# Splitting the weights of two hidden units for single-pass Hadamard products

## The chip, the core and the metric

The kernel runs on one core of a Trainium2 chip. The metric is the device time of one launch in microseconds (us): the median of three runs.

## What is computed

Eight sequences of 512 tokens with 512 features go through a layer norm, and from there along two ways whose results are multiplied.

```python
xn = _layernorm(x)
s = attention(xn)     # q, k, v; elu + 1; running sum of phi_k * v over the tokens; times phi_q; Wo
g = silu(ffn(xn))
return x + s * g

def ffn(x):                                        # HIDDEN 512, INTER 2048
    x = fwht(x * SU_ug) / SCALE
    x_up   = x @ W_up.T   * (Wscale_ug[:INTER] * SCALE)
    x_gate = x @ W_gate.T * (Wscale_ug[INTER:] * SCALE)
    x = silu(x_gate) * x_up
    x = fwht(x * SU_dp) / SCALE
    return x @ W_down.T * (Wscale_dp * SCALE)
```

`fwht` is a Walsh-Hadamard transform over the features. It is linear, so the kernel applies it to the weights once and not to the tokens. For a weight with 512 input features, held as four blocks of 128, it consists of butterflies between the blocks (additions and subtractions) and of a product with a 128 by 128 matrix `had` of +1 and -1 within each block.

## The kernel before

**Tiles and stages.** The tokens are taken in four passes `p` of two sequences each. All products are in float32. Each large product is done by a scheme of seven smaller ones (factors P1 to P7) on sums and differences of blocks. The operands of those factors are "encoded" by additions on VectorE or GpSimd, both for tokens and for weights. Pass 0 loads the raw weights, folds the transform into them, encodes them, uses them, and stores them to DRAM; passes 1 to 3 load the ready factors.

**Units.** The 2048 hidden features are cut into `NU` = 4 units `u`. Each unit needs the gate weights `f = u` and `u + 4` and the up weights `u` and `u + 4`. In pass 0 the units 0, 1 and 2 run through `gate` and `up` (lines 775 to 810), with weights made just ahead. Unit 3 uses `hidden_unit` (line 812) with a further level of the scheme, and its weights are made during the first `down` by `weights_ahead` (line 1061). `down` (line 858) runs after units 1 and 3.

**Making one folded weight** is `folded_w` (line 929). `raw_w` issues four loads on SP's queue. Then three steps are placed in time: `butterflies` (four VectorE operations of 128x512, lines 940 to 944), `fold` (two TensorE products of 128x512 with `had`, line 950, each result brought back from PSUM to the weight's tile by two ScalarE operations, line 955) and `encode` (four VectorE operations of 128x256, lines 312 to 315). The list at line 965 holds a place for each step: 5, 7 and 9.

**What sets the order.** The program is recorded in an order that `at` (line 429) and `advance` (line 434) make: a place is counted in TensorE products, and every step is recorded when its place has come. `get_w` (line 1112) places the steps of the next two weights: for the very next weight all of them, for the one behind it the first half. `later` and `pace` (lines 75 to 83) put side work behind groups of VectorE operations. Then a scheduler orders the instructions of each engine by priorities; on each engine they run strictly in that order. Products marked `keep_in_program_order` keep their place. SP issues the DMAs, one queue, in order too.

**Buffers.** `t8` is a pool of six tiles of 8 KB a partition, which gates, ups, attention operands, block outputs (`dn`, whose two tiles are stored to DRAM as `d_d` at the end of the first `down`) and the tiles of `weights_ahead` share. A new tile takes a slot that is free in the scheduler's view and waits for what last used it. `wpool` holds four weights. `xin` has one slot, in which the additional factors of the stored weights (`s_gate`, `s_up`, line 412) and the tokens of later sequences (`x`) follow each other. PSUM tag `t` has two banks, for the products with `had`; the folding of the down weights (`pwd`, line 1001) uses them too.

**Places that the prediction speaks of.** Line 460: the products of `gate` and `up` (`px_gate`, `pz_up` and so on; `px`, `py` and `pz` are PSUM banks). Line 476: VectorE's sums that read a `py` or `pz` bank (`g`, `u`). Line 470: ScalarE's copies of a `px` bank. Line 536: the products of `down`. Line 638: those of `hidden_unit`; line 648 the sums behind them. Line 93: the operations that `later` put off, here sums for the down weights (`rd`, `wd`). Line 140: the layer norm of the fourth sequence's tokens. Lines 710 and 711: ScalarE's elu of `q` (`neg_q`). Line 752: the store of `dn`.

Of the kernel before, what the change touches and what calls it, by code (L numbers as in the profile page):

```python
# [7 lines left out]

F32 = mybir.dt.float32
AF = mybir.ActivationFunctionType  # L10
ALU = mybir.AluOpType
PSUM = bass.MemoryType.PSUM
# [9 lines left out]
def kernel(  # L22
# [27 lines left out]
    nc = tc.nc  # L50
    P = 128
# [6 lines left out]
    NU = NG // 2  # L58
# [4 lines left out]
    const = ctx.enter_context(tc.tile_pool(name="const", bufs=1))  # L63
# [4 lines left out]
    t8 = ctx.enter_context(tc.tile_pool(name="t8", bufs=6))  # L68
# [5 lines left out]
    @contextmanager  # L74
    def background(behind=150):

        at = tc.cur_priority
        tc.cur_priority = at + behind
        yield
        tc.cur_priority = at  # L80
# [20 lines left out]

    cols_sb = const.tile([P, cols.shape[1]], F32, tag="cols", name="cols_sb")
    offs = {}
# [10 lines left out]

    bo_r = const.tile([P, D], F32, tag="bo_r", name="bo_r")
    ident = const.tile([P, P], F32, tag="ident", name="ident")
    had = const.tile([P, P], F32, tag="had", name="had")
    ones = const.tile([P, 1], F32, tag="ones", name="ones")
    su_ug = const.tile([P, KD], F32, tag="su_ug", name="su_ug")
    su_dp = const.tile([P, NF], F32, tag="su_dp", name="su_dp")  # L120
# [13 lines left out]
    def layernorm(b, xt, parts=1):  # L134
        n = NT // parts
        for i in range(0, NT, n):
# [6 lines left out]
            nc.vector.tensor_scalar(rstd, mv[:, :, 1], EPS, None, ALU.add)  # L143
            nc.scalar.activation(rstd, rstd, AF.Sqrt)
            nc.vector.reciprocal(rstd, rstd)
# [6 lines left out]
    def first_layernorms(xs):  # L152
# [8 lines left out]
        def pinned(ins):  # L161
            tc.keep_in_program_order(ins)

        for i in range(2 * NT + 1):
            if i < 2 * NT:
# [4 lines left out]
                pinned(nc.vector.tensor_scalar(r, mv[:, i, 1:2], EPS, None, ALU.add))  # L170
                nc.scalar.activation(r, r, AF.Sqrt)
            if i:
# [3 lines left out]
                if i <= NT:  # L176
                    pinned(nc.vector.scalar_tensor_tensor(n, m, -1.0, r, ALU.mult, ALU.mult))
                    nc.scalar.activation(x, x, AF.Identity, bias=n, scale=r)
                else:
# [3 lines left out]
    def normalized(b):  # L183
# [20 lines left out]
        def root():  # L204
            nc.vector.tensor_scalar(rstd, mv[:, :, 1], EPS, None, ALU.add)
            nc.scalar.activation(rstd, rstd, AF.Sqrt)

# [102 lines left out]
    def encode_weights(eng, w):  # L310
        w = w.rearrange("p j s e -> p s j e") if len(w.shape) == 4 else w
        eng.tensor_tensor(w[:, P5], w[:, P7], w[:, P4], ALU.add)
        eng.tensor_tensor(w[:, P6], w[:, P5], w[:, P1], ALU.subtract)
        eng.tensor_tensor(w[:, P3], w[:, P2], w[:, P6], ALU.subtract)
        eng.tensor_tensor(w[:, P7], w[:, P1], w[:, P7], ALU.subtract)
# [30 lines left out]
    def raw_w(name, src, n0, dn, step, c0, dc, w=None):  # L346

        w = new_w(name) if w is None else w
        for a in range(2):
            tiles = src[:, c0 + a * dc : c0 + a * dc + P].rearrange("(n p) e -> p n e", p=P)  # L350
            for b in range(2):
                n = n0 + b * dn
                place = (P1, P2, P7, P4)[2 * a + b]
                nc.sync.dma_start(w[:, :, place, :], tiles[:, n : n + step + 1 : step])
        return w
# [94 lines left out]
    def group(name, ws, rhs, dst, then, bias=(None, None), time=1.7):  # L450
# [14 lines left out]
        def snapshot(what, i):  # L465
# [5 lines left out]
            else:  # L471
                nc.scalar.activation(s, p, AF.Identity, bias=b)
            return s
# [218 lines left out]
    def attention(p, xo, co, get_w):  # L692
        def project(m, g, then):
# [4 lines left out]
            def whole(px):  # L698
                nc.scalar.activation(r[:, 0, 1], px, AF.Identity, bias=b[0])
                then(r)  # L700
# [225 lines left out]
    def folded_w(name, src, f, room=None):  # L926

        w = raw_w(f"{name}_{f}", src, 0, 2, 1, f * P, NG * P, room)
        places = (slice(P1, P7 + 1, 2), slice(P2, P4 + 1, 3))
        flat_w = w.rearrange("p j s e -> p (j s) e")  # L930

        def spots(at, *dims):
            o = flat_w[:, at : at + 1, :]
            return bass.AP(o.tensor, o.offset, [o.ap[0]] + [[step * P, 2] for step in dims] + [[1, P]])

        rs = [spots(0, 4, 2), spots(3, 8, 2)]

        def butterflies():
            a, b = (w[:, :, place, :] for place in places)
            nc.vector.tensor_tensor(spots(3, 7, 2), a, b, ALU.subtract)  # L940
            nc.vector.tensor_tensor(a, a, b, ALU.add)
            a, b = spots(0, 3, 2), spots(7, 3, 2)
            nc.vector.tensor_tensor(spots(4, 7, 2), a, b, ALU.subtract)
            nc.vector.tensor_tensor(a, a, b, ALU.add)

        def fold():
            for b in range(2):
                p = ps.tile([P, 2, 2, P], F32, tag="t", name=f"pw_{name}_{f}_{b}")
                tc.keep_in_program_order(
                    nc.tensor.matmul(  # L950
                        p, had, rs[b], start=True, stop=True,
                    )
                )
                for j in range(2):
                    nc.scalar.activation(
                        w[:, j, places[b], :], p[:, j], AF.Copy, scale=su_ug[:, 2 * b + j : 2 * b + j + 1]
                    )
        def encode():
            encode_weights(nc.vector, w)
            folded[name, f] = w  # L960
            if f >= NU:
                with background():
                    inner_w(name, f - NU, folded[name, f - NU], w)

        return w, [(5, butterflies), (7, fold), (9, encode)]

    folded = {}
    wd_f = dram.tile([FF, D], F32, tag="wd_f", name="wd_f")
# [74 lines left out]
    def first_w(m, g):  # L1043


        if m == "gate":
            return folded_w(m, wgate_t, g)
        if m == "up":
            return folded_w(m, wup_t, g)
        name, eng = f"{m}_{g}", nc.gpsimd if m == "o" else nc.vector  # L1050
        if m == "o":
            t = new_w(name)
            w = by_factor(t)
            rows_w(w, wo_t, g, 2)
        else:
            t = w = raw_w(name, sources[m], 0, 2, 1, g * P, 2 * P)

        def encode():
            encode_weights(eng, w)
            keep_w(name, t)  # L1060

        return w, [(5, encode)]
# [79 lines left out]
    had2 = t8.tile([P, P], F32, tag="t", name="had2")  # L1142
    src = ident
    for i in range(7):
        dst = had if i % 2 == 0 else had2
        s = src.rearrange("p (a t h) -> p a t h", t=2, h=1 << i)
        d = dst.rearrange("p (a t h) -> p a t h", t=2, h=1 << i)
        nc.gpsimd.tensor_tensor(d[:, :, 0, :], s[:, :, 0, :], s[:, :, 1, :], ALU.add)
        nc.gpsimd.tensor_tensor(d[:, :, 1, :], s[:, :, 0, :], s[:, :, 1, :], ALU.subtract)
        src = dst  # L1150
    xo = xop.tile([P, 7, 7, H], F32, tag="xo", name="xo_0")
    first_layernorms(xs)
    for b in range(2):
# [11 lines left out]
    rs = rd[:, : 3 * NF * P].rearrange("p (i c e) -> p i c e", i=3, e=P)  # L1165
# [141 lines left out]
```

## Time and profile before

| | |
|---|---|
| median of three runs | 1553.38 us (1552.45 to 1556.04) |
| the profiled execution | 1554.91 us |
| its span, first to last instruction | 1553.1 us |
| granted TensorE clock, mean | 0.999 |
| ScalarE busy (ACT) | 419.8 us (27%) |
| GpSimd busy (POOL) | 432.6 us (28%) |
| DMA | 273.31 MB, mean 176 GB/s |

The profile gives for each engine the time in which an instruction ran. Matmuls are pipelined, so the length printed for one is longer than the distance to the next; the distance between starts tells what a product costs. "PEld" are the weight loads of TensorE, which run beside its products. A row of a timeline has the start in us from the span's beginning, the length of the merged group, the engine, the line, the operation, the tiles, the shape and the count; in brackets, how long the engine was idle just before and what ended that. One float32 product of the program appears as two MATMUL records in the trace.

In pass 0, units 0 to 2 run from about 85 to 365 us. The products with `had` of the second unit (u = 1) lie between 181 and 225 us, those of `weights_ahead` between 263 and 286 us, and those of the third unit (u = 2) between 306 and 341 us.

### The profile page before, as it was taken

What the parts mean: (1) busy time and instruction counts of PE and PEld (TensorE: products, weight loads), DVE (VectorE), ACT (ScalarE), POOL (GpSimd) and SP (SyncE); (2) the same over time, 40 slices, a digit from 0 to 9 for tenths busy, and PEclk for the clock granted to TensorE, in tenths of its full rate; (3) what the DMA queues carried; (4) which work ended last, traced back from release to release, by engine and by line L of the source; (5) the groups of instructions that cost most, each with busy time, mean ns of one, the idle gap of its engine ahead of it and who ended that gap; (6) DMA issues with size and microseconds to landing.
All of it is one profiled execution on the core that took longest, in us unless ns stands there. A gap on an engine that the chain in (4) does not pass through costs nothing.

```text
span 1553.1 us, 15703 instructions
## 1 busy us (share of the span) xinstructions
PE 1524.6 (98%) x5924; PEld 1121.6 (72%) x5924; DVE 1006.7 (65%) x1423; ACT 419.8 (27%) x664; POOL 432.6 (28%) x236
## 2 busy tenths in 40 slices
PE   7989999999999999999999999999999999999998
PEld 3436446746874588888884488888886478888887
DVE  7989787467877665616767674715675575533673
ACT  4453341232125411112114431111213431111211
POOL 1231233004320161305511144302621126210731
PEclk9999999999999999999999999999999999999999
DMA  8345867797975244354576344335574233535462
GB/s 276 97 155 162 268 231 227 224 307 241 270 277 164 86 158 156 99 164 164 166 265 228 100 143 149 114 118 184 178 244 154 91 109 105 189 102 173 162 256 84
DMA packets 197692, 273.31 MB, mean 176 GB/s; under 512 B 56816, under 2 KB 155120, under 8 KB 193392
## 3 DMA queue, kind: packets, MB, share of 16 engines
q1 hardware_dynamic: 197472, 272.27, 53.3%
q8 instruction: 47, 0.77, 0.2%
q14 instruction: 29, 0.24, 0.1%
q10 hardware_dynamic: 144, 0.03, 0.0%
HBM read 196.25 MB, written 76.02 MB: 175 GB/s over the span
## 4 chain that ended last, share of the span: by engine, by line
PE 88%; DVE 7%; DMA 3%; ACT 1%; issue 1%; SPq 0%; POOL 0%; POOLq 0%; DVEq 0%; ACTq 0%
PE px_gu L638 19%; PE px_dn L536 13%; PE pz_gu L638 10%; PE pz_dn L536 7%; PE py_gu L638 5%; PE px_k L460 4%; PE py_dn L536 4%; PE px_o L536 4%; PE px_v L460 3%; PE px_q L460 3%; PE pz_o L536 2%; PE px_up L460 2%; PE pz_k L460 2%; PE pz_v L460 2%; PE pz_q L460 2%; PE px_gate L460 1%
## 5 line engine op out<-in xcount | busy, mean ns | idle before, releaser
L638 PE MATMUL px_gu<-xo,w_gu 128*128 128x256 f32 x1456 | 347.8, 380 | 2.4 <-DVE sb_gu L648 2.2
L638 PEld LDWEIGHTS px_gu<-xo,w_gu 128*128 128x128 f32 x1456 | 275.7, 190 | 47.3 <-issue 5.0
L536 PE MATMUL px_dn<-w_down,ho 128*128 128x256 f32 x1024 | 228.5, 379 | 0.0
L536 PEld LDWEIGHTS px_dn<-w_down,ho 128*128 128x128 f32 x1024 | 194.6, 190 | 28.2 <-issue 1.9
L638 PE MATMUL pz_gu<-xo,w_gu 128*128 128x256 f32 x728 | 187.7, 380 | 2.1 <-DVE u L476 1.6
L838 POOL TENSOR_TENSOR u<-u,v 128x1024 f32<-128x1024 f32 x26 | 61.0, 2369 | 366.3 <-DVE u L676 347.4
L638 PEld LDWEIGHTS pz_gu<-xo,w_gu 128*128 128x128 f32 x728 | 137.5, 190 | 23.3 <-DVE u L476 2.0
L536 PE MATMUL pz_dn<-w_down,ho 128*128 128x256 f32 x496 | 114.2, 383 | 3.4 <-DVE u L476 3.4
L536 PEld LDWEIGHTS pz_dn<-w_down,ho 128*128 128x128 f32 x496 | 95.0, 193 | 18.7 <-DVE u L476 3.8
L638 PE MATMUL py_gu<-xo,w_gu 128*128 128x256 f32 x364 | 93.4, 379 | 0.0
L304 POOL TENSOR_TENSOR co<-co 128x512 f32<-128x512 f32 x8 | 14.8, 1848 | 266.2 <-DVE co L737 266.2
L883 POOL TENSOR_TENSOR s<-s,d 128x512 f32<-128x512 f32 x30 | 40.0, 1335 | 165.5 <-ACT d L882 165.5
L638 PEld LDWEIGHTS py_gu<-xo,w_gu 128*128 128x128 f32 x364 | 69.2, 190 | 9.4
L842 POOL TENSOR_TENSOR v<-v,r 128x1024 f32<-128x1024 f32 x26 | 60.9, 2366 | 26.3 <-DVE r L676 25.5
L460 PE MATMUL px_k<-xo,w_k 128*128 128x512 f32 x128 | 62.2, 609 | 0.0
L460 PE MATMUL px_v<-xo,w_v 128*128 128x512 f32 x128 | 60.6, 594 | 0.0
L460 PE MATMUL px_q<-xo,w_q 128*128 128x512 f32 x128 | 60.3, 592 | 0.0
L828 ACT ACTIVATE a<-a,cols_sb 128x512 f32<-128x512 f32 x26 | 18.8, 724 | 152.2 <-DVE a L676 150.3
L882 ACT ACTIVATE d<-d 128x512 f32<-128x512 f32 x31 | 19.6, 632 | 144.4 <-DVE d L551 114.2
L536 PE MATMUL px_o<-w_o,co 128*128 128x256 f32 x256 | 58.4, 379 | 0.0
L828 ACT ACTIVATE u<-u,cols_sb 128x512 f32<-128x512 f32 x52 | 37.0, 722 | 78.1 <-DVE u L676 68.1
L536 PE MATMUL py_dn<-w_down,ho 128*128 128x256 f32 x256 | 57.9, 379 | 0.0
(269 smaller groups left out, 2416.2 us busy)
## 6 DMA issues: line engine op xcount, KB each, us to landing
w_gu<-d_gu SPq DMA_DIRECT2D x91, 896.0 KB, 4.4
w_down<-d_down SPq DMA_DIRECT2D x56, 512.0 KB, 4.1
d_s<-o SPq DMA_DIRECT2D x8, 1024.0 KB, 5.7
d_d<-dn SPq DMA_DIRECT2D x8, 1024.0 KB, 7.6
d<-d_d SPq DMA_DIRECT2D x8, 1024.0 KB, 5.6
s<-d_s SPq DMA_DIRECT2D x8, 1024.0 KB, 7.5
y<-in_x_dram SPq DMA_DIRECT2D x8, 1024.0 KB, 6.9
out_dram<-y SPq DMA_DIRECT2D x15, 512.0 KB, 3.3
```

The source lines that it names most:

```text
L304: eng.tensor_tensor(o[..., P5, :], o[..., P7, :], o[..., P1, :], ALU.subtract)
L460: nc.tensor.matmul(p.rearrange("p a t -> p (a t)") if len(r.shape) == 2 else p, ws[k][:, i, :], r, start=(first and k == 0), stop=(k == n ...
L536: nc.tensor.matmul(p[:, c], t[:, (2 * g + c) * P : (2 * g + c + 1) * P], ws[i](k), start=(first and k == 0 and c == cs[0]), stop=(k == n - ...
L638: nc.tensor.matmul(p[:, lane], w[:, lane, i, :], x[:, i, :], start=(first and lane == 0), stop=True, skip_group_check=True,)
L828: nc.scalar.activation(g[:, m], g[:, m], AF.Silu, scale=col("w_gate", u + m * NU + a * NG))
L838: nc.gpsimd.tensor_tensor(r[:, m], ru1[:, m], rv[:, m], ALU.add)
L842: nc.gpsimd.tensor_tensor(rv[:, m], rv[:, m], rr[:, m], ALU.add)
L882: nc.scalar.activation(d, d, AF.Silu)
L883: (nc.vector if final and (a, s) == (1, 0) else nc.gpsimd).tensor_tensor(r, r, d, ALU.mult)
```

## The change

For the weights with `f % 4` equal to 1 or 2 (gate and up weights 1, 2, 5 and 6, eight in all), the step `butterflies` also splits the result into two parts. ScalarE copies it into a tile of type float32r, which rounds it; VectorE subtracts the rounded part from the full one and writes the rest as float32r. Each half of the weight becomes two products with `had` in float32r, summed in PSUM. `had` holds +1 and -1, which are exact in that type, so its tile is declared float32r and read as float32 elsewhere. The two parts lie in a tile from the pool `t8`. For all folded weights, the second place of the list goes from 7 to 8.

```diff
-    had = const.tile([P, P], F32, tag="had", name="had")
+    had_r = const.tile([P, P], F32R, tag="had", name="had")
+    had = had_r.bitcast(F32)
...
+        parts = []
 
         def butterflies():
             a, b = (w[:, :, place, :] for place in places)
...
             nc.vector.tensor_tensor(a, a, b, ALU.add)
+            if f % NU in (1, 2):
+                t = t8.tile([P, 2, 2, 4 * P], F32R, tag="t", name=f"r_{name}_{f}")
+                for b in range(2):
+                    high, low = (
+                        t[:, b, i].rearrange("p (j a e) -> p j a e", j=2, a=2) for i in range(2)
+                    )
+                    nc.scalar.copy(high, rs[b])
+                    nc.vector.tensor_tensor(low, rs[b], high.bitcast(F32), ALU.subtract)
+                    parts.append(t[:, b])
+
+        def by_had(p, b):
+            if not parts:
+                tc.keep_in_program_order(nc.tensor.matmul(p, had, rs[b], start=True, stop=True))
+                return
+            for i in range(2):
+                tc.keep_in_program_order(
+                    nc.tensor.matmul(
+                        p.rearrange("p j a e -> p (j a e)"), had_r, parts[b][:, i], start=(i == 0), stop=(i == 1)
+                    )
+                )
 
         def fold():
             for b in range(2):
                 p = ps.tile([P, 2, 2, P], F32, tag="t", name=f"pw_{name}_{f}_{b}")
-                tc.keep_in_program_order(
-                    nc.tensor.matmul(
-                        p, had, rs[b], start=True, stop=True,
-                    )
-                )
+                by_had(p, b)
...
-        return w, [(5, butterflies), (7, fold), (9, encode)]
+        return w, [(5, butterflies), (8, fold), (9, encode)]
```

## The prediction, made before the changed kernel ran

> **What bounds the kernel now.** I read the shares of busy time first, then the chain of work that ended last, then what TensorE (PE) waited for in the window 60 to 400 us, in which the edit lies, and last the timelines of the engines at those waits. From the page:
>
> ```profile
> PE 1524.6 (98%) x5924; PEld 1121.6 (72%) x5924; DVE 1006.7 (65%) x1423; ACT 419.8 (27%) x664; POOL 432.6 (28%) x236
> ...
> PE 88%; DVE 7%; DMA 3%; ACT 1%; issue 1%; SPq 0%; POOL 0%; POOLq 0%; DVEq 0%; ACTq 0%
> ```
>
> TensorE is the bound, and the chain lies on it for 88%. So a product that is shortened is a gain, unless TensorE then waits. VectorE (DVE) is at 65% on average and ScalarE (ACT) at 27%; but the edit gives VectorE work in pass 0, and there it is the releaser of TensorE's waits. These, with the total, the times and the longest in us:
>
> ```profile
> PE pz_dn L536 <- DVE u L476: 3.4, 1, 3.4
> PE px_gate L460 <- DVE w_gate L313: 2.5, 2, 2.0
> PE px_gu L638 <- DVE sb_gu L648: 2.2, 1, 2.2
> ...
> PE pwd L1001 <- ACT w_gate L955: 1.7, 1, 1.7
> ```
>
> They sit at 258.71, 99.74, 381.88 and 106.83 us; a fifth, of 0.51, at 207.29. Each ends what an edit ahead of it gains or loses: where VectorE sets the end, TensorE coming earlier only waits longer.
>
> **The products.** TensorE's timeline:
>
> ```profile
> 194.60 1.88 PE L950 MATMUL pw_gate<-w_gate,had 128*128 128x512 f32 x4
> 196.32 1.88 PE L460 MATMUL pz_up<-xo,w_up 128*128 128x512 f32 x4
> ...
> 207.29 1.95 PE L460 MATMUL px_gate<-xo,w_gate 128*128 128x512 f32 x4 [0.51 <-DVE w_gate L313]
> ...
> 249.10 2.75 PE L536 MATMUL pz_dn<-w_down,ho 128*128 128x256 f32 x12
> ...
> 258.71 4.54 PE L536 MATMUL pz_dn<-w_down,ho 128*128 128x256 f32 x12 [3.41 <-DVE u L476]
> ...
> 381.88 1.13 PE L638 MATMUL px_gu<-xo,w_gu 128*128 128x256 f32 x4 [2.17 <-DVE sb_gu L648]
> ```
>
> The two products of one weight with `had` take 196.32 - 194.60 = 1.72 us, in four records of 0.43. No row shows a single-pass product of 128x512. Its price c is above that of a record with a quarter of the columns (the transposes of line 271: 128x128, four in 0.44, so 0.11) and not above one record of the same columns, 0.43. I take the middle, 0.27. A weight then costs 4 x 0.27 = 1.08 in place of 1.72: 0.64 less; eight weights 5.1 us less. With 0.11 it would be 10.2 less, with 0.43 nothing.
>
> The Trainium skill, page "FP8 and Floating Point Precision", section TensorE Precision Notes, says that true FP32 is done in four passes over high and low parts, and that reduced FP32 is read and truncated to FP22; from 0.86 us for a product, c would be about 0.215 (an estimate), the saving 6.9 and the sum below 0.7 lower.
>
> **The added work.** For a weight, two ScalarE copies of 128x512: the like copies of line 470 take 0.59 each, so 1.2 together. Two VectorE subtractions of 128x512: line 944 has 0.69 long and 0.60 from start to start, so 1.2. That is 9.6 us on each engine, in the units 1 and 2. What they cost is where they stand in the queues; I laid the changed program's instruction order against the times of before.
>
> *Unit 0, up to 110 us (no weight is split, but place 7 becomes 8): +0.9.* TensorE gets one more product of unit 0 ahead of `pw_gate_0`, so the wait at 99.74 (2.04) shortens to about 1.4. Then `pw_gate_4`'s second half needs the PSUM bank that ScalarE clears of `pwd_0`, and this eviction now stands behind the four `neg_q` operations: free at about 112.3, where TensorE comes at 107.8. So a wait of about 4.5 takes the place of the 1.70 at 106.83 and of two others (2.04 and 0.70, less the 1.4 left). 4.5 + 1.4 - 4.44 = 1.5, of which reordered products give back some; `py_gate_4` starts at 117.5 by my walk, 116.66 before: +0.9.
>
> *Unit 1, 110 to 260 us: +2.3 at its end.* VectorE and SP's queue (line 354 loads the raw weight, line 404 stores factors):
>
> ```profile
> 201.23 4.51 DVE L93 TENSOR_TENSOR rd<-rd 128x1024 f32<-128x1024 f32 x2
> 205.66 1.48 DVE L313 TENSOR_TENSOR w_gate<-w_gate 128x256 f32<-128x256 f32 x1
> ...
> 239.89 1.09 DVE L412 TENSOR_TENSOR s_up<-w_up 128x896 f32<-128x896 f32 x1 [3.67 <-DMA d_gu<-s_gate]
> ```
>
> ```profile
> 190.89 0.93 SPq L404 DMA_DIRECT2D d_gu<-s_up  x1
> 191.91 2.77 SPq L354 DMA_DIRECT2D w_up<-in_wup_t_dram  x4
> ```
>
> The 0.9 of unit 0 and the four subtractions of `r_gate_1` and `r_gate_5` (2.4), less about 1.0 of idle time that takes them up, put VectorE's `s_up` and so SP's store at 190.89 later by 2.3; the four loads of `w_up_1` stand behind it in the queue, so they land at 200.0 for 197.7. In the changed order the encoding of `w_gate_5` (205.66) stands behind two `rd` sums, the four butterflies of `w_up_1`, and the subtractions of `r_up_1`, which wait for ScalarE's copies: done at 211.9 for 207.1. TensorE needs it at 205.9, so the wait of 0.51 becomes about 6.0. The same delay runs on through x's layer norm, whose store on SP is at 224.7 (227.6 after, +2.9), to the chain of `xin`'s one slot: `s_gate`, its store, `s_up` (the 3.67 at 239.89), the loads behind it on SP, VectorE's butterflies of `w_gate_3`, and `u` (line 476), which releases `pz_dn` at 258.71. There `u` stands one operation (0.6) further ahead in the queue: 258.71 + 2.9 - 0.6 = 261.0, +2.3. TensorE comes at 257.7 (255.3 before), so what its cheaper products in unit 1 saved only lengthens or shortens a wait. If idle time takes up all additions, the end is -0.6; if it takes up none of the unit's eight subtractions (4.8), 0.9 + 4.8 - 0.6 = +5.1.
>
> The clock: after the wait of 3.41 the twelve `pz_dn` records take 4.54 where they take 2.75 at 249.10; the granted clock (PEclk, ninth column group) goes to 0.97 and 0.95:
>
> ```profile
> 160.00:180.00 20.00, 20.00 (x50) 9.33 (x50) 12.93 (x20) 9.41 (x28) 1.82 (x2) 1.00 0.90 298
> 240.00:260.00 20.00, 16.59 (x61) 11.76 (x60) 16.72 (x19) 1.76 (x3) 9.18 (x5) 0.97 0.94 284
> 260.00:280.00 20.00, 20.00 (x77) 15.10 (x77) 13.49 (x24) 5.57 (x13) 1.46 (x1) 0.95 0.57 164
> ```
>
> That is a loss of about 1.7. After the 2.04 at 99.74 there is none. The new waits of 4.5 and 6.0 may each cost 1.7 too, but both lie ahead of places where VectorE sets the end and TensorE has idle time to lose it in; and the wait at 258 stays near 3.3. So I add nothing, and keep +1.7 for the range.
>
> The skill's page "TensorE: Matmul & The Clock Gate", section Part 1: The HAM clock gate, speaks against the change here: by it an idle window of about 3.4 us halves the clock until a busy one has passed. The row of 4.54 for 2.75 agrees with a dip after 3.41; by the rule both new waits would bring one, by the rows only those beyond 2.04 might.
>
> *Unit 2, 300 to 345 us: -1.4.* `r_gate_2` takes the slot of a block output whose store is issued on SP at 300.49 and lands in 4.7 to 5.1 us (median 4.9), so at 305.4. Two copies and the last subtraction end at 307.4 to 308.1; TensorE comes at 306.21. Its waits, and the copies for `r_gate_6` that stand between the evictions of `pw_gate_2`'s two halves, make the factors behind come at 310.2 for 309.65: +0.55. The other three weights find their parts ready: 3 x 0.64 = -1.92. With c = 0.11 the sum is -3.3, with 0.43 it is +0.65.
>
> *Unit 3: -2.0.* At 381.88 TensorE waited 2.17 for `sb_gu`, which stood in VectorE's queue behind a layer norm that waited for its tokens:
>
> ```profile
> 379.95 1.29 DVE L140 BATCH_NORM_STATS2 st<-x 128x6 f32<-128x512 f32 x2 [3.48 <-DMA x<-in_x_dram]
> ```
>
> In the changed order those statistics come behind `sb_gu`, so that the wait goes. What is late next there is VectorE's own sums: about 0.2. If the wait stays, nothing is gained.
>
> *Behind 400 us* the order hardly changes, and TensorE waits little. **Sum**: +2.3 - 1.4 - 2.0 = -1.1 against the profiled execution (1554.91, span 1553.1 and 1.8 around it): 1553.8. The median of the runs, 1553.38, is 1.5 below that execution; the same -1.1 gives **1552.3**.
>
> **The rivals.** What a measurement can tell from no change is about 0.2%, 3.1 us.
>
> A, the forecast: the second unit swallows its gain, the third and fourth keep theirs. 1552.3, within 0.2%. Chance 0.36.
>
> B, faster: VectorE's idle time (35% on average) takes up all the additions in unit 1, so that the chain to `pz_dn` is not longer: -0.6 - 1.4 - 2.0 = -4.0, 1549.4. With c at 0.11, 1.9 less: 1547.5. For it: before its `s_up` VectorE waits 3.67 for a store. Against: that store is itself behind VectorE's earlier work. Chance 0.32.
>
> C, slower: VectorE's queue in unit 1 has no room where the chain needs it, so that all eight subtractions delay `u` and with it `pz_dn`, +5.1; and in unit 3 VectorE's own sums are late in place of the statistics, so that the 2.0 don't come: +5.1 - 1.4 = +3.7, 1557.1. It decides once the chain is later by more than 4.5 with nothing gained in unit 3 (4.5 - 1.4 = 3.1). For it: four of the five waits named end on VectorE, and its operations get longer beside others (line 313 took 1.48 at 205.66). Against: VectorE's idle time before `s_up`. Chance 0.26.
>
> D, the change doesn't do what it says: a product of the short type takes one record's 0.43, so that two cost as much as the float32 one: +2.3 + 0.65 - 2.0 = +0.95, 1554.3, within 0.2%. Chance 0.06.
>
> **The numbers.** Faster is B, 0.32; within 0.2% is A and D, 0.42; slower is C, 0.26. The range goes from B with the cheapest product, 1547.5, to just beyond C, 1558.0 (half of a clock dip of 1.7). A's own range is 1550.4 (c = 0.11) to 1556.1 (c = 0.43 and a dip: 2.05 + 1.7).
>
> **What would show it.** c is the distance of starts of the `had` products, against 0.43 a record. The walk is right if TensorE waits some 4.5 us for the bank at `pw_gate_4` near 108, some 6 for line 313's `w_gate` near 206, and still 3 to 4 at `pz_dn` near 258, resumed about 261; if `pw_gate_2` waits 1 to 2 us for VectorE's subtraction; and if no wait for `sb_gu` is left near 380. The forecast is wrong above all if `pz_dn` resumes before 259 (B) or beyond 263 (C), if the granted clock falls where it was 1.00, or if the loads behind SP's store at 190.89 are not what the encoding of `w_gate_5` follows.

## The result and the profile after

The changed kernel takes **1572.73 us** (median of five runs, 1569.21 to 1574.40); the kernel before takes 1553.38 (that median is of five runs, too). The ratio is 1.012, with a 95% interval of 1.0103 to 1.0136: **slower**, by 16 to 21 us. The forecast was 1552.3, the range 1547.5 to 1558.0. The prediction was wrong: even the rival on the slow side, C, at 1557.1, is 15.6 us too low.

The profiled execution took 1571.68 us with a span of 1569.9, so 16.8 more than that of before. The page of the changed kernel:

```profile
PE 1524.1 (97%) x5924; PEld 1124.1 (72%) x5924; DVE 1016.2 (65%) x1439; ACT 426.6 (27%) x680; POOL 427.9 (27%) x236
...
PE 88%; DVE 7%; DMA 2%; issue 1%; ACT 1%; SPq 0%; POOL 0%; POOLq 0%; DVEq 0%; ACTq 0%
```

These shares hardly differ from those of before: VectorE has 9.5 us more work, as the prediction counted (9.6), ScalarE 6.8 more (426.6 for 419.8; 9.6 were counted), and TensorE is still busy for 97%. A share of a whole span does not show 17 us. The waits of TensorE do; first the window 60 to 400 us, then what lies behind it:

```profile
PE px_gate L462 <- DVE w_gate L315: 10.0, 2, 8.2
PE pw_gate L960 <- ACT rd L1026: 4.3, 1, 4.3
...
PE px_gu L640 <- DMA w_gu<-d_gu: 2.0, 1, 2.0
PE pz_dn L538 <- DVE u L478: 1.3, 1, 1.3
```

```profile
PE px_dn L538 <- DMA w_down<-d_down: 7.6, 1, 7.6
```

(Lines stand 2 to 19 further down than before: 462 was 460, 538 was 536.) The wait for `sb_gu` is gone, as foreseen. The wait of 3.4 at `pz_dn` shrank to 1.3, where 3.3 was forecast. The waits of 4.3 and 8.2 were forecast as 4.5 and 6.0. The one of 7.6 was not; it lies at 452 us, behind all that was changed.

Where the time went is seen from how late TensorE is: for a moment of the trace of before, how much later the changed kernel has done the same amount of products (the split products counted like those that they replace). The starts of two traces differ by up to 1 us, so it is the steps from one column to the next that count.

| us in the trace before | 100 | 130 | 205 | 215 | 300 | 360 | 430 | 480 | 1520 |
|---|---|---|---|---|---|---|---|---|---|
| changed kernel, us late | -0.6 | 3.6 | 2.5 | 12.2 | 7.4 | 5.3 | 7.2 | 16.9 | 16.8 |

So unit 0 costs 4.2, the second unit 9.7 of which 4.8 come back, the third unit gains 2.1, unit 3 loses 1.9, and the second `down` loses 9.7. From 480 us on nothing changes any more. I call this number the lateness below; it is given for other kernels in the same way.

**The products.** TensorE's timeline of the changed kernel around the first split weight:

```profile
183.97 1.88 PE L462 MATMUL pz_up<-xo,w_up 128*128 128x512 f32 x4
185.29 1.49 PE L964 MATMUL pw_gate<-r_gate,had 128*128 128x512 f32 x4
186.62 1.88 PE L462 MATMUL pz_up<-xo,w_up 128*128 128x512 f32 x4
```

From 183.97 to 186.62 are 2.65 us. The four float32 records take 4 x 0.43 = 1.72 of it; 0.93 is left for the four single-pass products, **0.23 each** (0.27 was taken). A weight saves 0.79, eight save 6.3. The change does do what it says.

**The three waits and what follows each of them:**

```profile
112.28 2.08 PE L960 MATMUL pw_gate<-w_gate,had 128*128 128x512 f32 x2 [4.26 <-ACT rd L1026]
114.15 1.91 PE L1020 MATMUL pwd<-rd,had 128*128 128x512 f32 x2
115.86 1.91 PE L462 MATMUL px_gate<-xo,w_gate 128*128 128x512 f32 x2
117.56 2.00 PE L1020 MATMUL pwd<-rd,had 128*128 128x512 f32 x4
...
217.47 3.75 PE L462 MATMUL px_gate<-xo,w_gate 128*128 128x512 f32 x4 [8.15 <-DVE w_gate L315]
221.01 3.18 PE L462 MATMUL pz_gate<-xo,w_gate 128*128 128x512 f32 x4
223.62 1.48 PE L964 MATMUL pw_up<-r_up,had 128*128 128x512 f32 x4
...
267.33 2.86 PE L538 MATMUL pz_dn<-w_down,ho 128*128 128x256 f32 x12 [1.33 <-DVE u L478]
...
452.17 15.80 PE L538 MATMUL px_dn<-w_down,ho 128*128 128x256 f32 x64 [7.59 <-DMA w_down<-d_down]
```

Read the starts, not only the brackets. After the wait of 4.26 six records take from 112.28 to 117.56, 5.28 us, where six take 2.58: another 2.7 are lost. After the wait of 8.15 four records take 3.54 in place of 1.72, and the next four are slow in part; from 217.47 to 224.94 are 7.47 us for what takes 4.37 at full speed (1.72 + 2.65), so this dip costs 3.1. The table agrees: 9.7 lost there are 7.6 more of waiting (8.15 for 0.51), less one weight's 0.8, and 2.9 are left for the dip. After 7.59, 64 records take 15.6 (to 467.81) in place of 13.8. The granted clock (the number in front of the DMA share and GB/s) shows all three; in the trace of before it is 1.00 at these places:

```profile
100.00:120.00 20.00, 15.74 (x31) 6.58 (x30) 15.91 (x14) 11.85 (x25) 9.08 (x8) 0.83 0.37 120
200.00:220.00 20.00, 11.85 (x27) 5.21 (x26) 18.09 (x22) 5.57 (x12) 10.83 (x5) 0.83 0.83 288
450.00:470.00 20.00, 17.83 (x75) 15.42 (x76) 10.13 (x19) 3.17 (x4) 3.79 (x3) 0.86 0.56 219
```

**The loads of w_down.** SP's queue, first of the kernel before, then of the changed one, at the same point of the program:

```profile
419.38 0.45 SPq L916 DMA_DIRECT2D y<-in_x_dram  x1
421.87 2.05 SPq L339 DMA_DIRECT2D w_down<-d_down  x2
432.44 0.38 SPq L916 DMA_DIRECT2D y<-in_x_dram  x1
```

```profile
429.98 15.48 SPq L918 DMA_DIRECT2D y<-in_x_dram  x2
445.51 1.76 SPq L341 DMA_DIRECT2D w_down<-d_down  x3
```

Before, two loads of `w_down` stood between the two `y`. Now both `y` stand ahead of all three. The second `y` takes the tile of the transposed tokens `z` of the fourth sequence, and waits until VectorE has read them; three loads, of which two went ahead of it before, wait behind it, 15 us. This order was fixed when the program was built; the prediction did not follow it that far.

### The profile page after: what moved, and what is told of

Its sections match the earlier page's. It is cut to its first block, busy times and chain, and to the rows that moved or that the text cites. A ratio compares the mean times of both kernels' runs of the same rounds, so it can differ in the third digit from the quotient of the medians.

```text
span 1569.9 us, 15738 instructions
## 1 busy us (share of the span) xinstructions
PE 1524.1 (97%) x5924; PEld 1124.1 (72%) x5924; DVE 1016.2 (65%) x1439; ACT 426.6 (27%) x680; POOL 427.9 (27%) x236
## 4 chain that ended last, share of the span: by engine, by line
PE 88%; DVE 7%; DMA 2%; issue 1%; ACT 1%; SPq 0%; POOL 0%; POOLq 0%; DVEq 0%; ACTq 0%
PE px_gu L640 19%; PE px_dn L538 12%; PE pz_gu L640 10%; PE pz_dn L538 6%; PE py_gu L640 5%; PE px_k L462 4%; PE py_dn L538 4%; PE px_o L538 4%; PE px_v L462 3%; PE px_q L462 3%; PE px_gate L462 2%; PE pz_o L538 2%; PE px_up L462 2%; PE pz_k L462 2%; PE pz_q L462 2%; PE pz_v L462 2%
## 5 line engine op out<-in xcount | busy, mean ns | idle before, releaser
L538 PEld LDWEIGHTS pz_dn<-w_down,ho 128*128 128x128 f32 x496 | 93.9, 190 | 15.6 <-DVE u L478 1.7
```

Source lines behind the costliest of these rows:

```text
L538: nc.tensor.matmul(p[:, c], t[:, (2 * g + c) * P : (2 * g + c + 1) * P], ws[i](k), start=(first and k == 0 and c == cs[0]), stop=(k == n - ...
```

## The experiments

My theory after this reading: three places lose time independently of each other, (1) the PSUM bank in unit 0, (2) VectorE's late encoding in unit 1, (3) SP's order in the second `down`, each with a dip of the clock. The first rival: all of it is one thing, the added work that makes VectorE late, carried on. Each ratio is against runs of the kernel before on the same chip (medians 1553.75 to 1555.85).

### The place of the fold alone

The kernel before with `(8, fold)` for `(7, fold)`, for all folded weights, for unit 0 alone, for unit 1 alone; nothing is split.

```diff
-        return w, [(5, butterflies), (7, fold), (9, encode)]
+        return w, [(5, butterflies), (8, fold), (9, encode)]                         # place8_only
+        return w, [(5, butterflies), (8 if f % NU == 0 else 7, fold), (9, encode)]   # place8_unit0
+        return w, [(5, butterflies), (8 if f % NU == 1 else 7, fold), (9, encode)]   # place8_unit1
```

> The kernel before with the fold at place 8 instead of 7 and no weight split. Theory (three separate places cost the time: the PSUM bank behind neg_q in unit 0, VectorE's late encoding in unit 1, and SP's queue in the second down): only the first is here, a wait of about 4.3 us near 108 us at pw_gate_4 with a clock dip behind it, +3.5 us at 130 us. Half or more of it stays to the end: 1554 to 1557. No wait over 3 us near 207 and none at px_dn near 450. Rival (the added VectorE and ScalarE work makes all of the loss, the place is innocent): 1552 to 1554.

Measured: 1564.91, ratio 1.0060 (1.0045 to 1.0075). More than either expectation. The wait of 4.26 and its dip are there (2.2 late at 130 us), but also a wait of 6.45 for `w_gate` at 215 us, with no weight split. That fell outside my theory: I had put the second wait down to the added work. So I asked which unit's place makes it.

> The kernel before, fold at place 8 for the first unit's weights only. VectorE's built order in unit 1 is that of before. Theory (unit 1's wait comes from the order that place 8 makes there): +2.6 at 130 us from the wait for the PSUM bank and its clock dip, a wait for w_gate of less than 2 near 207, and part of it given back at pz_dn: 0 to +3 us against the kernel before. Rival (unit 1's wait is unit 0's lateness carried on by VectorE): a wait of 5 or more near 210 us, +7 to +9.

> The kernel before, fold at place 8 for the second unit's weights only: VectorE's four encodings of w_gate_5 then stand behind both rd sums and w_up's butterflies, as in place8_only. Theory: no loss up to 200 us, a wait of 5 to 7 for w_gate near 210 us with a clock dip, +5 to +8 against the kernel before. Rival: less than 2 us of wait there, 0 to +2.

Measured: unit 0 alone 1556.33, ratio 1.0017 (1.0008 to 1.0027); unit 1 alone 1559.87, ratio 1.0043 (1.0029 to 1.0056). TensorE of place8_unit0, then of place8_unit1:

```profile
111.29 2.07 PE L950 MATMUL pw_gate<-w_gate,had 128*128 128x512 f32 x2 [4.26 <-ACT rd L1007]
...
209.43 1.95 PE L460 MATMUL px_gate<-xo,w_gate 128*128 128x512 f32 x4 [0.33 <-DVE w_gate L313]
```

```profile
212.26 3.75 PE L460 MATMUL px_gate<-xo,w_gate 128*128 128x512 f32 x4 [5.95 <-DVE w_gate L313]
```

In place8_unit0 unit 0's lateness (2.3 us at 205) does not lengthen the wait at 209. In place8_unit1 nothing is late up to 205 (-0.5), and the wait is 5.95. The theory holds for both: the places are separate, and 2.6 and 6.7 us add up to place8_only's 9.3. What place 8 does in unit 1 lies in VectorE's queue. VectorE's built order in the two kernels from `w_up`'s first butterfly on (the rows of w_gate are the encoding that TensorE waits for):

```
place8_unit0 (as before): w_up, w_up, w_gate L312, w_up, u, w_up, rd,      w_gate L313, L315, L314, g
place8_unit1:             w_up, u, w_up, rd, w_up, rd, w_up, w_gate L312, w_up, w_gate L313, L315, L314, g
```

In both orders the encodings from L313 on stand behind `w_up`'s four butterflies, `u` and two `rd`; one product later only one operation more stands in front, 0.6 us. What differs more is how long the operations take. VectorE of place8_unit0, then of place8_unit1:

```profile
201.57 0.68 DVE L943 TENSOR_TENSOR w_up<-w_up 128x512 f32<-128x512 f32 x1
...
207.80 1.48 DVE L313 TENSOR_TENSOR w_gate<-w_gate 128x256 f32<-128x256 f32 x1
```

```profile
205.22 1.75 DVE L943 TENSOR_TENSOR w_up<-w_up 128x512 f32<-128x512 f32 x1
...
211.70 0.41 DVE L313 TENSOR_TENSOR w_gate<-w_gate 128x256 f32<-128x256 f32 x1
```

From the first butterfly to L313 are 7.9 us in place8_unit0 (from 199.90) and 11.6 in place8_unit1 (from 200.09): two butterflies take 1.7 for 0.7, and two `rd` 5.5 for 4.4. They stand beside GpSimd's operations there (201.87 to 210.29); in place8_unit0 the encodings do, and take 1.48 for 0.41. And the first butterfly itself waits 2.65 for its load, so that it comes 2.3 later than in the kernel before (197.76), although TensorE is 0.5 early. So the order moves which operations fall into GpSimd's stretch and when the load is issued. That GpSimd makes them long was not tested.

### The second unit's split alone, at place 7

```diff
-            if f % NU in (1, 2):
+            if f % NU == 1:
```

and `(7, fold)`. In unit1_extra_work the condition in `by_had` is `if True`, so the float32 products stay; in unit1_no_subtraction the subtraction is left out and both products of a half read the rounded part, so that the output lacks the small part.

> The changed kernel with only the second unit's weights split (f % 4 == 1) and the fold at place 7. Theory: the wait for VectorE's encoding of w_gate_5 near 207 us is there, 6 to 8 us and a clock dip of 2 to 3 us, about +9; the wait at pz_dn near 258 gives some 4 back, the four cheaper weights 3; end about +3 to +5, 1556 to 1559, and w_down's loads of the second down are in time. Rival (all loss comes with VectorE's lateness, whichever unit): the wait at px_dn near 450 us is there too, 1562 or more.

Measured: 1562.60, ratio 1.0048 (1.0033 to 1.0063), so +7.5; the waits are there and `w_down` is in time, but the end lies above the expected 1556 to 1559. The kernel's ScalarE and TensorE:

```profile
205.59 1.14 ACT L954 CAST r_up<-w_up 128x512 fp32r<-128x512 f32 x2 [5.89 <-DVE w_up L947]
206.64 0.58 ACT L472 COPY sc_gate<-px_gate 128x512 f32<-128x512 f32 x1
```

```profile
207.27 3.53 PE L462 MATMUL px_gate<-xo,w_gate 128*128 128x512 f32 x4 [2.96 <-ACT sc_gate L472]
...
214.83 3.42 PE L462 MATMUL px_gate<-xo,w_gate 128*128 128x512 f32 x4 [4.03 <-DVE w_gate L315]
```

Here is a wait that I had not counted at all: ScalarE's copies for `r_up` wait 5.89 for VectorE's butterflies, and behind them in ScalarE's queue stands the eviction `sc_gate` that frees TensorE's bank.

> Second unit only, fold at place 7: copies and subtractions are made, but the products use the unsplit float32 weights as before (the parts are not used). Theory (the added ScalarE and VectorE work makes both waits near 207 us): waits of 2 to 3 for sc_gate and about 4 for w_gate, as in unit1_place7, end 0 to 3 us above it: 1562 to 1565. Rival (the waits come from TensorE being earlier, so from the cheaper products): no wait over 1 us there, 1554 to 1557.

Measured: 1564.33, ratio 1.0057 (1.0041 to 1.0074), waits of 2.99 and 5.58. The theory: the added work makes the waits, not the earlier TensorE.

> Second unit only, fold at place 7: ScalarE's copies are made, VectorE's eight subtractions are left out, and each half is multiplied twice by its rounded part, so the low part is missing from the output. Theory (VectorE's subtractions make the stored factors s_up late, SP's loads of w_up behind that store late, and with them both waits): the loads land near 198 us, both waits shrink to under 1 us, 1551 to 1555. Rival (ScalarE's copies for r_up, queued in front of the eviction sc_gate, make the wait by themselves): a wait of 2 to 3 for sc_gate near 205 us stays, 1557 to 1560.

Measured: 1559.10, ratio 1.0024 (1.0015 to 1.0033). Half right. The wait for `sc_gate` falls to 0.51 and VectorE's first operation on `w_up` comes at 198.64 (201.96 in unit1_place7), but waits of 2.24 for `w_gate`, 1.80 for `sb_gate` (ScalarE) and 5.17 at `pz_dn` are left. Of the 7.5 us the subtractions make about half; the rest, 3.7, comes with ScalarE's copies and the order that they bring, which I did not take apart further.

### The third unit's split alone, and who is in front of w_down

```diff
-            if f % NU in (1, 2):
+            if f % NU == 2:
```

and `(7, fold)`.

> The changed kernel with only the third unit's weights split (f % 4 == 2) and the fold at place 7. Theory: TensorE is not late up to 300 us; unit 2 gains 2 to 3 us; then SP's queue holds the loads of w_down behind the second y, whose tile comes free late: a wait of some 7.5 us near 435 to 450 us, a clock dip of 2.3, and about 1 before, so +8: 1560 to 1563. Rival (that wait only shows the delay that TensorE and VectorE bring along from units 0 and 1): no wait over 2 us there and a gain, 1549 to 1552.

Measured: 1564.95, ratio 1.0062 (1.0047 to 1.0077). TensorE is 3.2 us ahead at 360, 0.5 behind at 430, and 10.0 behind at 480, after a wait of 7.33 for `w_down`. TensorE comes to this point on time; so that wait is not carried lateness, and the first rival falls. Next, is it the order on SP?

```diff
-        nc.sync.dma_start(y, x[2 * p + s].rearrange("(n p) d -> p n d", p=P))
+        with background(50 if (p, s) == (0, 1) else 0):        # y_behind
+            nc.sync.dma_start(y, x[2 * p + s].rearrange("(n p) d -> p n d", p=P))
...
+        eng = nc.gpsimd if (p, s) == (0, 1) else nc.sync       # the two y_on_gpsimd
+        eng.dma_start(y, x[2 * p + s].rearrange("(n p) d -> p n d", p=P))
```

y_behind and both_y_on_gpsimd are the whole change with this edit, unit2_y_on_gpsimd is unit2_place7 with it.

> The changed kernel, with the load of y for the second sequence of pass 0 recorded at a lower priority, so that SP issues it behind two of the three loads of w_down, as the kernel before does. Theory (SP's order makes the wait of 7.6 at px_dn): the wait and its clock dip go, 10 to 11 us less than the changed kernel: 1560 to 1563. Rival (the loads are late because everything is, or the DMA queues are fuller): 1570 to 1573.

Measured: 1566.41, ratio 1.0071 (1.0054 to 1.0088): between the two. The wait of 7.6 at `px_dn` is gone, but a wait of 2.23 for `sa_k` and a dip at 474 us take 4.1 back: in this order the load of the next `x` fell behind, too.

> Only the third unit's weights split, fold at place 7, and the load of y for the second sequence of pass 0 issued by GpSimd instead of SP, so that it stands in front of no load of w_down. Theory: the wait of 7.3 at px_dn goes with its clock dip, and unlike in y_behind the load of x stays where the kernel before has it; what is left is unit 2's gain less the waits of 375 to 435 us: 1 to 3 us below the kernel before, 1552 to 1554. Rival (y is late for whoever issues it, and GpSimd's products s*silu(d) now stand behind it): a wait moves to px_k near 470 us, 1557 to 1561.

> The whole change, with that one load of y issued by GpSimd. Theory: the waits of units 0 and 1 stay, the 10 to 11 us near 430 to 480 go: 1560 to 1563. Rival (the loss of y_behind near 474 us belongs to any such move): 1566 to 1569.

Measured: 1560.75, ratio 1.0033 (1.0020 to 1.0045), and 1569.89, ratio 1.0087 (1.0072 to 1.0102). The first lies in its rival's range (1557 to 1561), the second 0.9 above its rival's (1566 to 1569). No load of `w_down` is late, yet a wait of 3.3 and 3.5 for `sa_k` comes in its place: GpSimd issues `y` at 440.23 (SP did at 432.44 before), VectorE waits for it, and its last sums and ScalarE's stand ahead of `sa_k`. VectorE of unit2_y_on_gpsimd:

```profile
450.62 0.69 DVE L886 TENSOR_TENSOR y<-y,s 128x512 f32<-128x512 f32 x1 [3.87 <-DMA y<-in_x_dram]
```

So SP's order is not the whole cause: with it mended, 4 to 5 us are still lost behind 430 us (by the lateness, 4.1 in y_behind, 5.2 and 5.4 in these two, 9.5 in unit2_place7). `y` itself is late, because the tile that it takes is read late.

### The cause behind it: the layer norm of the fourth sequence

Followed back in the traces: `y` waits for VectorE's transposes of `z`, `z` for the stored tokens `d_x`, and `d_x` for the layer norm of `x_3`. That is the layer norm whose statistics, in the changed order, come behind `sb_gu`; the prediction had booked this as a gain of 2.0. The load of its tokens is issued later, too. SP of the kernel before, SP of the changed one, and VectorE of the changed one:

```profile
368.75 0.77 SPq L129 DMA_DIRECT2D x<-in_x_dram  x1
...
396.36 0.37 SPq L190 DMA_DIRECT2D d_x<-x  x1
```

```profile
379.92 0.38 SPq L131 DMA_DIRECT2D x<-in_x_dram  x1
...
410.98 0.37 SPq L192 DMA_DIRECT2D d_x<-x  x1
```

```profile
389.80 0.68 DVE L142 BATCH_NORM_STATS2 st<-x 128x6 f32<-128x512 f32 x1
```

The statistics come at 389.80 for 379.95, the store 14.6 later, where TensorE is 5 to 9 later. The test records that layer norm at a higher priority and changes nothing else; the first two kernels are unit2_place7 with it, the third is the whole change, the last the kernel before:

```diff
-                    with background():
+                    with background(100):          # 50 in unit2_norm_earliest
                         normalized(3)
```

> Only the third unit's weights split, fold at place 7, and the layer norm of the fourth sequence (line 1251, x_3) recorded 100 instead of 150 priorities behind. In the built order SP then stores d_x of x_3 ahead of two loads, and the second y stands behind two of the three loads of w_down again, as in the kernel before. Theory (the late layer norm of x_3 starts the chain d_x, z, transposes, y, w_down that ends in the wait of 7.3): that wait and the one at px_k of unit2_y_on_gpsimd go, the gain of unit 2 stays in part: 1 to 3 us below the kernel before, ratio 0.998 to 0.9995. Rival (the wait moves again, since the cheaper products only let TensorE come early): 3 us or more above it.

> The same with 50 in place of 100: d_x of x_3 is stored one load earlier still. Theory: as unit2_norm_earlier, within 1 us of it; if VectorE's statistics now stand in front of sb_gu near 380 us, up to 2 more. Rival: 3 us or more above the kernel before.

> The whole change with that layer norm 100 instead of 150 priorities behind. Theory: of the 17 us lost, the waits of units 0 and 1 stay (6 us at 300 us) and the 10 to 11 near 430 to 480 go: 1559 to 1562. Rival (both_y_on_gpsimd: a wait at px_k comes in its place): 1566 to 1570.

> Control: the kernel before with only that layer norm 100 instead of 150 priorities behind. Its built order differs from before's in one place of SP's queue (the store of x_3 stands one load earlier). Both theories: within 1 us of the kernel before.

Measured: unit2_norm_earlier 1556.64, ratio 1.0015 (1.0006 to 1.0024); unit2_norm_earliest 1557.02, 1.0017 (1.0005 to 1.0029); both_norm_earlier 1565.52, 1.0076 (1.0060 to 1.0091); the control 1555.85, 1.0009 (1.0000 to 1.0018). Neither wait, for `w_down` or for `sa_k`, is left in unit2_norm_earlier: by the ratios 7 us of that kernel's loss of 9.6 go with that priority (0.0047), and 7 of the whole change's 19 (0.0044). both_norm_earlier lies between its expectation (1559 to 1562) and its rival's, and the control 1.4 us above the kernel before where at most 1 was expected; its trace has a wait of 1.81 for `w_down` at 424.98 that the kernel before has not.

What the edit moves is not the statistics. VectorE and SP of unit2_place7, then of unit2_norm_earlier:

```profile
383.09 0.68 DVE L142 BATCH_NORM_STATS2 st<-x 128x6 f32<-128x512 f32 x1
404.27 0.37 SPq L192 DMA_DIRECT2D d_x<-x  x1
```

```profile
383.66 0.68 DVE L142 BATCH_NORM_STATS2 st<-x 128x6 f32<-128x512 f32 x1
400.44 0.37 SPq L192 DMA_DIRECT2D d_x<-x  x1
```

The statistics come as late as without it. It is the second half of the layer norm that comes earlier: the store by 3.8 us, VectorE's first transposes of `z` by 7.6 (423.96 for 431.61), and SP again issues two loads of `w_down` ahead of the second `y`. So the loss behind 430 us hangs on how far back this layer norm is recorded, and the gain at `sb_gu` does not need it (there is no wait for it near 380 us in unit2_norm_earlier either); which of the three moves counts was not taken apart.

The expected gain is not there either: TensorE is 2.7 us ahead at 360 and 2.4 behind at 376. Why?

> As unit2_norm_earlier, but VectorE's subtractions are left out and each half is multiplied twice by its rounded part, so the low part is missing from the output. Theory (TensorE, 3 us early, only waits for what VectorE and the stores of s_up set in unit 3): the waits of 1.5 (u), 1.1 (u) and 2.0 (w_gu) between 360 and 375 us stay within 0.5 each, and the gain is lost there as before: 0 to +2 us against the kernel before. Rival (the subtractions make VectorE late in unit 3): these waits go and 2 to 4 us are gained.

> As unit2_norm_earlier, but of the third unit's weights only the two gates are split (gain of the products 1.6 instead of 3.2). Theory (unit 3's start is set by VectorE and the stores of s_up): the waits at 360 to 375 us get shorter by what TensorE comes later, the end stays at -1 to +2 us against the kernel before. Rival (the up weights' copies and subtractions, next to s_up, are what makes unit 3 late): no wait over 1 us for w_gu, 1 to 2 us gained.

Both are unit2_norm_earlier with an edit. In unit2_no_subtraction the subtraction is left out as in unit1_no_subtraction; in unit2_gates_only the condition is `if f % NU == 2 and name == "gate"`. Measured: unit2_no_subtraction 1553.95, ratio 1.0003 (0.9994 to 1.0012); unit2_gates_only 1552.22, ratio 0.9990 (0.9981 to 0.9999). TensorE of unit2_no_subtraction:

```profile
359.98 1.98 PE L462 MATMUL pz_up<-xo,w_up 128*128 128x512 f32 x4 [1.47 <-DVE u L478]
...
364.79 1.13 PE L640 MATMUL pz_gu<-xo,w_gu 128*128 128x256 f32 x4 [1.10 <-DVE u L478]
...
370.48 2.83 PE L640 MATMUL px_gu<-xo,w_gu 128*128 128x256 f32 x8 [1.98 <-DMA w_gu<-d_gu]
```

Without VectorE's subtractions TensorE is 5.4 us ahead at 360, and the same three waits, 1.47, 1.10 and 1.98, leave 0.4 of it at 376 (a dip is in it: 2.63 for eight records that take 1.73). So the subtractions don't make these waits. With only the gates split these waits are 0.83, 1.10 and none, and a small gain is left. The measured -1.5 us lies outside my -1 to +2, and in the rival's 1 to 2 us gained; that the wait for `w_gu` is gone is the rival's sign as well. TensorE comes only 1.3 later there at 360 (1.4 ahead for 2.7), less than the 2.06 that went. So what the up weights bring, their copies and the order on SP, which shifted there, too, has a part in that wait; my theory, that TensorE is merely too early, does not cover it. The interval (-3.0 to -0.2 us) does not settle how large each part is.

### Together, and a version that is faster

> The whole split (both units) with the fold at place 7 and the layer norm of x_3 at 100. Theory (three separate places, of which the first and third are now gone): unit 1's waits for sc_gate and w_gate near 207 us stay, as in unit1_place7; unit1_place7 and unit2_norm_earlier add up to about +9 us against the kernel before, ratio 1.004 to 1.007. Rival (the wait in unit 1 comes from place 8 alone): ratio under 1.003.

> unit2_gates_only with the layer norm of x_3 where the kernel before has it (150 behind): only the two gates of the third unit are split, nothing else is changed. TensorE's built order is the same, VectorE's differs in one place. Theory: 0 to 3 us below the kernel before, ratio 0.998 to 1.000, as unit2_gates_only. Rival (its gain belongs to the earlier layer norm): ratio 1.000 to 1.003.

Measured: both_place7_norm 1563.15, ratio 1.0046 (1.0033 to 1.0059), with waits of 2.91 for `sc_gate` and 5.57 for `w_gate` near 207 us: unit 1 keeps its loss. It differs from both_norm_earlier in the place alone (1.0046 for 1.0076). So by the ratios the whole change's loss of 18.6 us is about 6.8 for the layer norm's priority, 4.7 for place 8 and 7.1 for what is left, unit 1's split in the main (7.5 alone). unit2_gates_norm150, which is the kernel before with only two weights split, place 7 and nothing else, 1554.40, ratio **0.9988** (0.9979 to 0.9997): 0.5 to 3.3 us faster than the kernel before by the interval, where its products save 1.6. It is a small gain: its one trace shows TensorE 0.3 us ahead from 480 us on, and two dips in front of that.

## Why the prediction was wrong

- **"Behind 400 us the order hardly changes": the step that failed most.** It was an assumption; SP's order there changed, and 9.7 us were lost between 430 and 480. Its root lies next to the step "Unit 3: -2.0": the wait for `sb_gu` did go, because the statistics of a layer norm were put behind it, but the rest of that layer norm came later as well, and its chain (`d_x`, `z`, transposes, `y`, `w_down`) the prediction did not follow. The experiments with that layer norm's priority show it: 7 us by the ratios, with the statistics as late as without the edit. What remains of unit 3's own account is +1.9 for the forecast -2.0: the waits for `u` and `w_gu` came in place of the one for `sb_gu`.
- **"So I add nothing" for the clock: failed.** The two waits in units 0 and 1 cost 2.7 and 3.1 more, the one at 452 us 1.8. The dip after `pz_dn` (1.7) did vanish. The argument was that VectorE sets the end there and that TensorE has idle time to lose it in. The Trainium skill's page "TensorE: Matmul & The Clock Gate", section Part 1: The HAM clock gate, whose rule was weighed against the change, was the better guide: the runs show dips after all three.
- **Unit 0, +0.9: the wait right, the sum not.** 4.26 for about 4.5, TensorE there at 108.0 for 107.8; the other wait kept 1.89 where 1.4 was forecast. The step of 4.2 in the table is about that wait and the unpriced dip, less two waits that went (4.26 + 2.7 - 1.70 - 0.70 = 4.6). place8_unit0 shows that unit 0's place alone ends at +1.2 to +4.2.
- **Unit 1, +2.3 at its end: the mechanism right, the size off.** The term that was mis-sized is the 2.3 by which VectorE's last `s_up` and SP's loads of `w_up` were to be late. That `s_up` came at 197.69 for 189.16, 8.5 later: 3.1 came with unit 0 (0.9 forecast), the four subtractions took 3.5 (2.4 forecast), and the rest, 2.0, is other operations that took longer (a butterfly 2.72 for 0.69, two encodings 1.49 and 1.38 for 0.42), less idle time. So `w_up`'s loads landed at 204 for 200.0. The encoding did come behind `rd`, the butterflies and `r_up`'s subtractions, and the wait was 8.15 for 6.0. The chain to `pz_dn` followed: the layer norm's store was issued at 235.14 for the 227.6 forecast, and `pz_dn` resumed at 267.3 for 261.0. TensorE, forecast there at 257.7, came at 266.0, so 1.33 of wait is left: VectorE still sets the end, but sums and encodings in front of that layer norm in its queue read what TensorE makes, and TensorE was late by the wait and the dip.
- **What the change part by part means.** The prediction laid unit 1's loss at the added work. Of the loss, place 8 alone makes as much (+6.7) as the split alone does at place 7 (+7.5). They do not add up: the lateness rises by 4.9 over the whole change's unit 1 (from 205 to 300 us). Why not was not tested.
- **Unit 2, -1.4: right.** -2.1 with c = 0.23 for 0.27: the first weight gained nothing (0.2 late, 0.55 forecast), the other three 0.79 each for 0.64. But "keeps its gain" failed: unit 3 takes it back (unit2_no_subtraction).
- **Rival C** named the right side and, in part, the right place (VectorE's queue in unit 1), with 5.1 as its worst; it lacked the dips and SP's queue. B fell with the wait at 207. D fell: 0.23.

## What to carry to other kernels

When the order of queues is built by a scheduler, an edit that frees an engine early also moves loads and side work elsewhere; walk the built order of every queue, the DMA queue above all, to the end of the stage behind the last moved instruction, and treat a side task that moves later as a debt whose chain must be followed until somebody needs it. A wait of 4 us or more on TensorE is to be priced with a dip of its clock behind it, 1.5 to 3.1 us here, and a wait of 2 to 4 us may bring one. A saving of TensorE ahead of a point that another engine sets is worth nothing there: split only what comes ahead of a point that TensorE sets, here two weights and not eight.

## What the runs showed of the hardware

- A single-pass product of 128x512 takes 0.23 us where the float32 one takes 0.86, so two of them cost 0.54 of it.
- The length of a wait does not alone decide whether the clock dips. In these runs, every wait of 4.0 us or more cost about 1.5 to 3.1 behind it. At 99 us a wait of 2.22 cost nothing in one kernel, and one of 2.16 cost about 1.2 on its four records in another; at `pz_dn` 3.28 cost nothing and 2.70 cost 1.7. TensorE of unit1_place7 and both_place7_norm, then of both_y_on_gpsimd and place8_unit0:

```profile
99.90 1.95 PE L462 MATMUL px_gate<-xo,w_gate 128*128 128x512 f32 x4 [2.22 <-DVE w_gate L315]
```

```profile
98.99 3.20 PE L462 MATMUL px_gate<-xo,w_gate 128*128 128x512 f32 x4 [2.16 <-DVE w_gate L315]
```

```profile
268.09 2.86 PE L538 MATMUL pz_dn<-w_down,ho 128*128 128x256 f32 x12 [3.28 <-DVE u L478]
```

```profile
260.14 4.54 PE L536 MATMUL pz_dn<-w_down,ho 128*128 128x256 f32 x12 [2.70 <-DVE u L476]
```

What decides is where the wait falls. In every trace, up to the end of the program, the granted clock goes to 0.50 in steps of 3.41 us: in the changed kernel the dips start at 110.97, 213.37 and 448.89, which are 30 and 69 steps apart, and last 2, 3 and 2 steps. Steps laid over the two places at 99 us, of both_place7_norm, then of unit1_place7 (the first number behind the comma is TensorE's busy time, the one in front of the DMA share the granted clock):

```profile
96.14:99.56 3.42, 1.26 (x4) 0.36 (x3) 3.42 (x6) 1.97 (x2) 2.42 (x2) 1.00 0.07 31
99.56:102.97 3.41, 3.41 (x6) 1.35 (x5) 3.41 (x4) 0.00 (x0) 0.00 (x0) 0.50 1.01 362
```

```profile
94.92:98.33 3.41, 2.76 (x7) 0.95 (x5) 3.41 (x3) 0.61 (x1) 3.41 (x3) 1.00 0.00 0
98.33:101.75 3.42, 1.85 (x5) 0.92 (x6) 3.42 (x6) 1.36 (x2) 1.15 (x1) 1.00 0.46 189
101.75:105.16 3.41, 3.41 (x9) 1.27 (x7) 3.22 (x4) 0.16 (x1) 0.00 (x0) 1.00 1.06 335
```

The wait of 2.16 lies in one step, and the next step runs at half the clock. The wait of 2.22 is cut into 0.65 and 1.57, and none follows. At `pz_dn` the 2.70 lies in one step, the 3.28 is cut into 1.65 and 1.63. Counted so from 80 to 1500 us in the traces of all twenty kernels: each of the 46 full-speed steps in which TensorE waits for 1.98 us or more is followed by a slow one, and none of those with 1.90 or less; of five from 1.92 to 1.96 two are. A wait of 4 us puts at least 2.0 into one step wherever it falls, which fits that all of these cost something.

The same section of the Trainium skill's page says that the window in which idleness is counted runs freely. The traces agree: the steps lie at other places of the program in each execution. But a step here need not be idle for the whole 3.4 us by which the prediction weighed the change; 1.98 are enough.
